# A Mamba-and-experts layer on one core: two chunks' head products in one group

## The chip, the core and the metric

The kernel runs on one core of a Trainium2 chip. Its engines work at the same time and wait for each other by semaphores: TensorE (PE, matrix products into PSUM; its weight loads are listed apart as PEld), VectorE (DVE), ScalarE (ACT), GpSimd (POOL) and SyncE (SP, which here only issues DMAs). PSUM has eight banks of 128 partitions by 512 numbers; a product is written into a bank by PE and read out by DVE or ACT before the bank can be used again. The metric is the device time of one execution in microseconds. A run's "span" is the time from the first to the last instruction in the profile.

## What is computed

Eight sequences of 2048 tokens with 256 features go through one layer: a state-space mixer (Mamba-2) behind a modulated layer norm, then a dense mixture of eight experts behind another. All is float32. Cut to what matters here:

```python
h = _layernorm(x) * (1 + ca) + sa
zxbcdt = h @ W_in                       # z: 512, xBC: 768, dt: 8 columns
xBC = silu(causal_conv4(xBC))           # x: 8 heads of 64, B: 128, C: 128
dt = softplus(dt + dt_bias); A = -exp(A_log)
# the scan, in chunks; cs = cumsum(dt * A) in a chunk
y_diag = sum_j (C_i . B_j) exp(cs_i - cs_j) [j <= i] dt_j x_j
y_off  = exp(cs_i) C_i . S_prev          # S_prev: state that earlier chunks left
S      = exp(cs_last) S_prev + sum_j B_j exp(cs_last - cs_j) dt_j x_j
y = (y_diag + y_off + x * D) * silu(z)
x = x + ga * ((y * rsqrt(mean(y * y) + EPS) * norm_w) @ W_out)
h = _layernorm(x) * (1 + cb) + sb
w = softmax(h @ gate_w + gate_b); w = w * (w >= 0.1); w = w / sum(w)
x = x + gb * sum_e w_e * (h @ expert_w[e] + expert_b[e])
```

The kernel may take its own chunk length, since the result doesn't depend on it: it uses 128 tokens.

## The kernel before

**Tiling.** The tokens are cut into 32 blocks of 512 (`n`), four to a sequence. A block has four chunks of 128 tokens (`c`). Feature-major tiles (features on partitions, tokens along the free axis) serve the projections and the convolution, token-major ones the norms and the experts. The state of a sequence is handed from chunk to chunk in `carry["state"]`.

**Emission.** The order in which instructions are written down comes from a plan: every stage of a block is a Python generator that is put on a list of events at a planned time, in estimated microseconds, and each `yield t` puts the rest of it `t` later on that list. `run()` takes the events in order. `PERIOD` is 70, so stages of several blocks interleave: while block n is projected, the output product of block n-1 and the experts of blocks n-2 and n-3 are written down between its parts. `STARTS` gives each stage's start within its block's plan. The planned times only decide the order; on the chip each engine runs its own queue in order and waits where an operand is missing. The framework under it may still exchange independent instructions on an engine, so the order that counts is that of the built program.

**PSUM.** `take(use, count)` gives a bank that the plan holds to be free and waits in the plan otherwise; `MOST` limits how many banks one use may hold (experts "ex" 3, projections "pj" 2, head products "y" 1, the rest "m" 4). `give` frees it 3.0 planned us later. On the chip the next writer waits for the last reader's semaphore.

**The stages of a block.**
- `fetch` (L241) issues the load of the block's tokens on SP (L105), into one of four buffers; a buffer is free when the store of its earlier block (L737) has landed. `first_norm` takes the statistics (L315, L316 on DVE); `modulated` computes 1/sqrt on POOL (L310, L311), the shift on DVE (L324), the normalised rows on ACT (L328), their transposes on PE (L338) and the modulation on ACT (L340).
- `project_xbc`: six groups of two products of 512 columns (L409); for each, `conv` takes the bank, ACT does the first tap (L364) and saves the last three columns (L368), DVE does the other three taps (L372). `silu_xbc` (L427) follows.
- `steps_of_time`: dt's products, which use 32 columns of the array (L459); softplus and the cumulative sum on DVE and ACT (L471 to L489); `cs` goes to DRAM (L492); dt, cs and e are transposed to token-major by PE (L497) and read out by DVE (L502).
- `project_z`: four groups (L445), read out by ACT with a SiLU (L432).
- `spread` loads, for each chunk, cs of all heads on all partitions (L512, SP) into half of a tile `wide`.
- `within`, for each chunk: ACT writes relu(cs differences) for each head into the other half of `wide` (L526), PE transposes x and B (L536, L537) and makes C.B (L539), ACT takes exp of both halves in one instruction of 2048 columns (L540). DVE makes `xdt` (L543), `sm`, `bm` and the decayed scores `w` (L561), POOL `xdec` (L556) and `cw` (L564). When the state of the chunk before is there, PE does the head products (L579): for each of eight heads `xdt` by `w`, then `state` by `cw`. A head has 64 columns, so such a product uses half of the array's columns, and the two heads of a pair go to the two halves. All of them go to one PSUM bank. Then come the chunk's contribution to the state (L587, full width), the state's update on POOL (L590) and DVE (L609, L607), and the read-out of y: four DVE instructions that add D x (L600), one that multiplies by the gate (L603), the square on ACT (L616) and two sums on POOL (L618, L619).
- `output` sums the squares over partitions on PE (L633), takes 1/sqrt, and does the output product per chunk (L648); `residual` adds it on DVE (L657) with new statistics.
- `gate_weights`: second norm, the gate's logits (L675, 32 columns of the array), a transpose (L683), the softmax and threshold on DVE, and the transpose of the weights `wt` (L714).
- `experts`: bias (L750), then for each chunk four groups of two products of 512 columns (L761); `weighted` adds each expert's part on DVE (L724). After the last one POOL scales and adds the result to the rows (L732, L734), and SP stores the block (L737).

## Time and profile before

| | us |
|---|---|
| median of 4 runs | 2453.53 |
| lowest and highest | 2449.8, 2457.21 |
| the profiled execution | 2451.29 |
| its span | 2449.5 |
| granted TensorE clock, mean | 0.994 |

| group | count | busy us | mean ns |
|---|---|---|---|
| L761 experts, PE | 2048 | 966.1 | 596 |
| L409 projection xBC, PE | 768 | 366.6 | 600 |
| L579 head products, `wide` by `xdt`, PE | 2048 | 142.5 | 281 |
| L579 head products, `cw` by `state`, PE | 1920 | 127.0 | 274 |
| L724 weighting of experts, DVE | 1024 | 485.2 | 476 |
| L600 y plus D x, DVE | 512 | 178.8 | 349 |
| L603 y times gate, DVE | 128 | 87.1 | 681 |
| L540 exp, 128x2048, ACT | 128 | 244.3 | 1908 |
| L564 `cw`, POOL | 128 | 350.6 | 2739 |

How to read it: a float32 product is listed as two records on PE, and records overlap, since a matmul's shown end lies after the start of the next one; so the sum of the means is more than the time they take, and the step from start to start is what counts. "128*64" in a record is the part of the array that is used (rows by columns), "128x512" the output. A row of waits reads: who waited (engine, what it writes, line), for whom, us in total, how often, the longest. "Issue" means that nothing in the profile held the engine back.

### The profile page before, as it was taken

How to read it: one execution, taken by the hardware profiler on the slowest of the kernel's cores; microseconds unless marked ns; L12 is line 12 of the kernel's file. 1: busy time of each engine (PE TensorE's matmuls, PEld its weight loads, DVE VectorE, ACT ScalarE, POOL GpSimd, SP SyncE). 2: the span in 40 equal slices, each digit the busy share in tenths (PEclk: the TensorE clock that was granted, in tenths of full speed). 3: DMA queues.
4: the chain of work that ended last, by engine and by line, in shares of the span. 5: the costliest groups of instructions: out<-in, count | busy, mean ns of one | idle time of the engine just before them, and what ended most of it. 6: DMA issues, size and time to landing. Idle time of an engine off the chain costs nothing.

```text
span 2449.5 us, 33770 instructions
## 1 busy us (share of the span) xinstructions
PE 2365.5 (97%) x11602; PEld 1328.5 (54%) x11602; DVE 1845.9 (75%) x4414; ACT 1508.1 (62%) x2739; POOL 1136.0 (46%) x1244
## 2 busy tenths in 40 slices
PE   7899999999999999999999999999999999999998
PEld 4555555555555555555555555555555555555554
DVE  5767787778777787876777777788777777777775
ACT  6766666666666566656666666666666666656630
POOL 3544454444444544544444445444444544454441
PEclk9899999999999999999999999999999999999999
DMA  5101101111111111011111011110111111111100
GB/s 154 44 28 52 46 28 49 48 45 45 44 37 45 44 53 45 28 53 44 45 45 52 29 45 44 53 45 28 53 44 45 45 45 37 45 44 53 36 26 17
DMA packets 64601, 110.51 MB, mean 45 GB/s; under 512 B 7048, under 2 KB 47024, under 8 KB 64432
## 3 DMA queue, kind: packets, MB, share of 16 engines
q1 hardware_dynamic: 64416, 108.35, 13.2%
q8 instruction: 93, 1.52, 0.3%
q14 instruction: 76, 0.62, 0.1%
q10 hardware_dynamic: 16, 0.01, 0.0%
HBM read 89.47 MB, written 18.87 MB: 44 GB/s over the span
## 4 chain that ended last, share of the span: by engine, by line
PE 27%; DVE 24%; ACT 20%; POOL 14%; DMA 7%; issue 3%; ACTq 0%; POOLq 0%; SPq 0%; DVEq 0%
PE bank L761 10%; POOL cw L564 7%; DVE xbc L372 7%; DMA wide<-cs_d 6%; ACT wide L526 5%; PE bank L445 5%; ACT wide L540 5%; DVE res L724 3%; PE bank L579 3%; PE bank L409 3%; DVE bank L600 3%; ACT xn L328 2%; POOL rstd L311 2%; PE bank L750 2%; POOL xdec L556 2%
## 5 line engine op out<-in xcount | busy, mean ns | idle before, releaser
L761 PE MATMUL bank<-we_sb,ht 128*128 128x512 f32 x2048 | 966.1, 596 | 1.4 <-ACT wide L540 1.4
L761 PEld LDWEIGHTS bank<-we_sb,ht 128*128 128x128 f32 x2048 | 375.8, 191 | 385.1 <-issue 367.4
L724 DVE SCALAR_TENSOR_TENSOR res<-bank,wt,res 128x256 f32<-128x256 f32 x1024 | 485.2, 476 | 100.8 <-PE bank L761 83.2
L564 POOL TENSOR_TENSOR cw<-wide,xbc 128x1024 f32<-128x1024 f32 x128 | 350.6, 2739 | 307.1 <-ACT wide L540 235.3
L372 DVE SCALAR_TENSOR_TENSOR xbc<-bank,conv_w_sb,xbc 128x509 f32<-128x509 f32 (+2 forms) x576 | 425.9, 741 | 50.2 <-ACT halo L368 47.9
L526 ACT ACTIVATE wide<-wide,tok_major 128x128 f32<-128x128 f32 x1024 | 325.1, 389 | 189.4 <-DMA wide<-cs_d 167.7
L409 PE MATMUL bank<-ht,w_in_sb 128*128 128x512 f32 x768 | 366.6, 600 | 6.8 <-DVE zs L603 5.6
L328 ACT ACTIVATE xn<-xt,shift,rstd 128x256 f32<-128x256 f32 x256 | 132.9, 589 | 289.8 <-DVE shift L324 289.8
L590 POOL TENSOR_TENSOR state<-state,wide 128x512 f32<-128x512 f32 x112 | 118.7, 1060 | 336.8 <-DVE state L609 301.4
L540 ACT ACTIVATE wide<-wide 128x2048 f32<-128x2048 f32 x128 | 244.3, 1908 | 1.0
L648 PE MATMUL bank<-wo,zs 128*128 128x256 f32 x1024 | 243.7, 382 | 0.0
L600 DVE SCALAR_TENSOR_TENSOR bank<-xbc,d_ch,bank 128x128 f32<-128x128 f32 x512 | 178.8, 349 | 83.2 <-PE bank L579 77.2
L445 PE MATMUL bank<-ht,w_in_sb 128*128 128x512 f32 x512 | 241.2, 593 | 0.0
L648 PEld LDWEIGHTS bank<-wo,zs 128*128 128x128 f32 x1024 | 196.0, 192 | 79.5 <-issue 52.5
L618 POOL TENSOR_TENSOR sq<-sq 128x256 f32<-128x256 f32 x128 | 96.0, 750 | 280.9 <-ACT sq L616 278.7
L409 PEld LDWEIGHTS bank<-ht,w_in_sb 128*128 128x128 f32 x768 | 139.7, 192 | 157.7 <-issue 147.1
L561 DVE TENSOR_TENSOR wide<-wide,sm 128x1024 f32<-128x1024 f32 x128 | 200.3, 1565 | 0.0
L556 POOL TENSOR_TENSOR xdec<-xdt,tok_major 128x512 f32<-128x512 f32 x120 | 138.8, 1157 | 114.4 <-DVE xdt L543 83.3
L364 ACT ACTIVATE xbc<-bank,conv_b_sb,conv_w_sb 128x512 f32<-128x512 f32 x192 | 147.0, 766 | 59.7 <-PE bank L409 59.6
L445 PEld LDWEIGHTS bank<-ht,w_in_sb 128*128 128x128 f32 x512 | 95.7, 192 | 109.0 <-issue 106.4
L579 PEld LDWEIGHTS bank<-wide,xdt 128*64 128x64 f32 x2048 | 110.9, 138 | 68.6 <-issue 32.6
L732 POOL TENSOR_TENSOR res<-res,gates 128x256 f32<-128x256 f32 x128 | 96.1, 751 | 105.2 <-DVE res L724 105.2
(127 smaller groups left out, 3171.3 us busy)
## 6 DMA issues: line engine op xcount, KB each, us to landing
wide<-cs_d SPq DMA_DIRECT2D x128, 512.0 KB
xt<-_attn_hidden_states_dram SPq DMA_DIRECT2D x32, 512.0 KB
out_dram<-xt SPq DMA_DIRECT2D x32, 512.0 KB
we_sb<-in_L_ffn_expert_w_dram SPq DMA_DIRECT2D x8, 256.0 KB
cs_d<-cs SPq DMA_DIRECT2D x32, 64.0 KB
ht<-in_L_wmod_dram SPq DMA_DIRECT2D x2, 512.0 KB
w_in_sb<-in_L_attn_W_in_dram SPq DMA_DIRECT2D x1, 776.0 KB
w_in_sb<-in_L_attn_W_in_dram SPq DMA_DIRECT2D x1, 512.0 KB
```

Of the source, the lines that this page charges most:

```text
L372: nc.vector.scalar_tensor_tensor(acc[:, ahead:], ps[:, : T - ahead], conv_w_sb[:, m, k : k + 1], acc[:, ahead:], ALU.mult, ALU.add,)
L409: nc.tensor.matmul(ps, w_in_sb[:, k, DI + m * P : DI + (m + 1) * P], ht[:, k, :], start=(k == 0), stop=(k == KD - 1),)
L445: nc.tensor.matmul(ps, w_in_sb[:, k, ts(m, P)], ht[:, k, :], start=(k == 0), stop=(k == KD - 1),)
L526: nc.scalar.activation(wide[:, 1, h, :], wide[:, 0, h, :], AF.Relu, bias=tok_major[:, 1, c, h : h + 1])
L540: nc.scalar.activation(wide, wide, AF.Exp, scale=-1.0)
L556: nc.gpsimd.tensor_tensor(by_head(xdec), by_head(xdt), per_head(tok_major[:, 2, c, :]), ALU.mult)
L561: nc.vector.tensor_tensor(w, w, sm[:, None, :].to_broadcast([P, NH, P]), ALU.mult)
L564: nc.gpsimd.tensor_tensor(cw, up_to, ct_[:, None, :].to_broadcast([P, NH, P]), ALU.mult)
L600: nc.vector.scalar_tensor_tensor(y[:, m, :], xbc[:, m, tok], d_ch[:, m : m + 1], y[:, m, :], ALU.mult, ALU.add)
L648: nc.tensor.matmul(o_ps[:, :DM], d["zs"][:, m, ts(c, P)], wo[:, m, :], start=(m == 0), stop=(m == MI - 1),)
L724: nc.vector.scalar_tensor_tensor(res, ps[:, ts(q, DM)], wt[:, c, e + q : e + q + 1], res, ALU.mult, ALU.add)
L761: nc.tensor.matmul(ps, ht[:, k, ts(c, P)], we_sb[:, k, e : e + per, :].rearrange("p e o -> p (e o)"), start=(k == 0), stop=(k == KD - 1),)
```

## The change

The head products leave `within` and move into a new generator `outputs`, which is started behind every second chunk and handles both chunks of the pair. It takes two PSUM banks at once and writes down all head products of the first chunk and then of the second, one behind the other; then the read-out of the first bank and that of the second, with the same instructions as before. The state's contribution and update of a chunk now come ahead of its head products. `wide` is cut in two tiles: `wide` (two buffers) and `w` (three), so that exp becomes two instructions of 1024 columns. `xdt` and `cw` have three buffers, `state` four.

In the plan, the transposes of dt come 3.0 later, the transpose of the gate's weights 2.5 later, the sum of squares 3.5 later, `fetch` starts 8 later, `gate_weights` 4 later and `experts` 9 later.

```diff
-    MOST = {"ex": 3, "pj": 2, "y": 1, "m": 4}
+    MOST = {"ex": 3, "pj": 2, "y": 2, "m": 4}
...
         nc.scalar.activation(e, cs, AF.Exp, bias=whole)
-        yield 4.0
+        yield 7.0
         t_ps = yield from take("m")
...
-        wide = info[n]["wide", c] = new(chk, [P, 2, NH, P], "wide")
+        wide = info[n]["wide", c] = new(chk, [P, NH, P], "wide")
...
+        w = new(chk, [P, NH, P], "w", bufs=3)
         for h in range(NH):
             nc.scalar.activation(
-                wide[:, 1, h, :], wide[:, 0, h, :], AF.Relu, bias=tok_major[:, 1, c, h : h + 1]
+                w[:, h, :], wide[:, h, :], AF.Relu, bias=tok_major[:, 1, c, h : h + 1]
             )
...
         nc.scalar.activation(wide, wide, AF.Exp, scale=-1.0)
+        nc.scalar.activation(w, w, AF.Exp, scale=-1.0)
         yield 1.2
-        xdt = new(chk, [P, DI], "xdt")
+        xdt = new(chk, [P, DI], "xdt", bufs=3)
...
-        cw = new(chk, [P, NH, P], "cw")
-        nc.gpsimd.tensor_tensor(cw, up_to, ct_[:, None, :].to_broadcast([P, NH, P]), ALU.mult)
+        cw = new(chk, [P, NH, P], "cw", bufs=3)
+        nc.gpsimd.tensor_tensor(cw, wide, ct_[:, None, :].to_broadcast([P, NH, P]), ALU.mult)
...
         if not last:
 
             st_ps = yield from take("m")
             nc.tensor.matmul(st_ps[:, :DI], bm, xdec, start=True, stop=True)
-            behind = new(blk, [P, DI], "state", bufs=3)
+            behind = new(blk, [P, DI], "state", bufs=4)
...
         d["state", c] = True
+        d["parts", c] = [(xdt, w)] if state is None else [(xdt, w), (state, cw)]
+        yield 1.5
         if not last:
             if state is None:
                 nc.vector.tensor_copy(behind, st_ps[:, :DI])
             else:
                 nc.vector.tensor_add(behind, st_ps[:, :DI], behind)
             give(st_ps)
...
+        if c % 2:
+            yield 1.5
+            yield from outputs(n, c - 1)
+
+    def outputs(n, first):
+
+        d = info[n]
+        xbc, g = d["xbc"], d["zs"]
+
+        pair = yield from take("y", 2)
+        for j, y_ps in enumerate(pair):
+            parts = d["parts", first + j]
+            for i, (lhs, rhs) in enumerate(parts):
+                for h in range(NH):
+                    m, q = divmod(h, 2)
+                    nc.tensor.matmul(
+                        y_ps[ts(q, HEADDIM), ts(m, P)], lhs[:, ts(h, HEADDIM)], rhs[:, h, :],
+                        start=(i == 0 and m == 0), stop=(i == len(parts) - 1),
+                        skip_group_check=True,
+                    )
+        yield from until(d, *(("z_silu", m) for m in range(MI)))
+        for j, y_ps in enumerate(pair):
+            c = first + j
+            tok = ts(c, P)
+            yield 1.4
+            y = y_ps.rearrange("p (m t) -> p m t", m=MI)
+            for m in range(MI):
+                nc.vector.scalar_tensor_tensor(
+                    y[:, m, :], xbc[:, m, tok], d_ch[:, m : m + 1], y[:, m, :],
+                    ALU.mult, ALU.add,
+                )
+            nc.vector.tensor_tensor(g[:, :, tok], y, g[:, :, tok], ALU.mult)
+            give(y_ps)
+            yield 1.8
...
@@ def output
         wo = gated[b][0]
+        yield 3.5
         s_ps = yield from take("m")
...
@@ def gate_weights
         nc.vector.tensor_mul(w, w, over(wsum))
-        yield 4.0
+        yield 6.5
...
-        (fetch, -20.0), (first_norm, -9.0), (project_xbc, 11.5), (project_z, 42.0),
-        (silu_xbc, 47.5), (output, 128.0), (gate_weights, 151.0), (experts, 183.0),
+        (fetch, -12.0), (first_norm, -9.0), (project_xbc, 11.5), (project_z, 42.0),
+        (silu_xbc, 47.5), (output, 128.0), (gate_weights, 155.0), (experts, 192.0),
```

The lines of the changed kernel that the text names: L608 head products (before L579), L576 the state's contribution (L587), L579 and L590 its update (L590, L609), L620 and L624 the read-out of y (L600, L603), L740 the weighting (L724), L777 the experts (L761), L748, L750 and L753 the result and its store (L732, L734, L737), L527 the relu (L526), L541 and L542 the two exps (L540), L565 `cw` (L564), L664 the output product (L648), L691, L699 and L730 the gate's products and transposes (L675, L683, L714).

## The prediction, made before the changed kernel had run

> **What bounds the kernel now.** I read the page's busy shares first, then the stretch between fill and drain by windows, then the waits of TensorE, then its timeline.
>
> ```profile
> PE 2365.5 (97%) x11602; PEld 1328.5 (54%) x11602; DVE 1845.9 (75%) x4414; ACT 1508.1 (62%) x2739; POOL 1136.0 (46%) x1244
> 200.00:2380.00 2180.00, 2134.15 (x10564) 1198.90 (x10563) 1669.96 (x4007) 1358.55 (x2469) 1032.38 (x1113) 1.00 0.13 44
> PE bank L497 <- DVE xbc L372: 23.8, 29, 1.5
> PE bank L714 <- DVE wt L710: 11.1, 14, 1.6
> PE bank L338 <- DVE zs L603: 6.0, 10, 0.8
> PE bank L409 <- DVE zs L603: 5.6, 13, 0.7
> ```
>
> TensorE (PE) is the bound. Between 200 and 2380 us it is busy 2134.15 of 2180 us at clock 1.00, so 45.9 us are idle, and the four rows of waits (total, times, longest) make 46.5 us over the whole run: nearly all of it. Nothing else waits long enough to matter; the 75% of DVE counts only where it ends these four waits. So two things can move the time: the time that the same matmuls take, and these stops.
>
> The timeline shows what a matmul costs (start, shown length, records). Shown lengths overlap; the step from one start to the next is the cost.
>
> ```profile
> 1209.88 1.88 PE L761 MATMUL bank<-we_sb,ht 128*128 128x512 f32 x4
> 1211.60 1.89 PE L648 MATMUL bank<-wo,zs 128*128 128x256 f32 x8
> 1213.42 1.09 PE L579 MATMUL bank<-wide,xdt 128*64 128x128 f32 x16
> 1214.44 1.13 PE L587 MATMUL bank<-xdec,bm 128*128 128x512 f32 x2
> 1215.41 1.88 PE L761 MATMUL bank<-we_sb,ht 128*128 128x512 f32 x4
> 1217.12 1.89 PE L648 MATMUL bank<-wo,zs 128*128 128x256 f32 x8
> 1229.18 0.64 PE L459 MATMUL bank<-ht,w_dt 128*32 128x128 f32 x16
> 1229.76 1.09 PE L579 MATMUL bank<-wide,xdt 128*64 128x128 f32 x16
> 1230.68 1.04 PE L579 MATMUL bank<-cw,state 128*64 128x128 f32 x16
> 1231.66 1.13 PE L587 MATMUL bank<-xdec,bm 128*128 128x512 f32 x2
> 1232.62 1.88 PE L761 MATMUL bank<-we_sb,ht 128*128 128x512 f32 x4
> ```
>
> The column 128*64 is the width of the array that is used. Between full-width groups eight L648 records take 1.72 us and four of L761 1.71 to 1.72. Ahead of a narrow group the eight take 1.82. Sixteen narrow records would take 0.875 (two halves of the array at once, 0.109 a pair: the four transposes of L536 take 0.43 to 0.44); the first sixteen take 0.92 and the last sixteen of a group 0.98. L587, half of 1.72, should take 0.86 and takes 0.96 to 0.97 behind a narrow group. Medians over all such places: 0.093 + 0.045 us to go narrow, 0.093 + 0.103 us to come back: 0.139 and 0.196. L459 shows the same (0.58 for 0.44 of work), and narrow to narrow (L459 to L579) costs 0.141.
>
> **The change, part by part.**
>
> *Grouping.* No matmul is added or removed (6458 in both programs). I counted changes of width along PE's order in both: into narrow from full 164, after 134; back 164, after 134; narrow to narrow 32, after 1. It is not half of them, because the new groups no longer sit next to L459's and L675's narrow groups, which now go in and out alone. Saving 30 x 0.139 + 30 x 0.196 + 31 x 0.141 = 4.2 + 5.9 + 4.4 = **14.4 us**. The groups of two are whole in the new order (four runs of eight, one behind the other). If a change of width were only moved into a weight load, the saving would be 0; each piece above is a step between starts, so I take all of it.
>
> *The stop at L497.* The wait names the last tap of the convolution, not dt:
>
> ```profile
> 1242.41 0.60 PE L338 MATMUL bank<-ident,xn 128*128 128x128 f32 x4
> 1244.09 0.30 PE L497 MATMUL bank<-ident,dt 128*128 128x128 f32 x1 [1.08 <-DVE xbc L372]
> 1243.21 0.74 DVE L372 SCALAR_TENSOR_TENSOR xbc<-bank,conv_w_sb,xbc 128x511 f32<-128x511 f32 x1
> ```
>
> dt was ready (L483 at 1239.24); what lacked is the PSUM bank, which L497 takes over from L409 and which DVE still read until 1243.95. DVE has no gap from 1232.67 to there. A stop costs its idle time and the 0.16 us by which a shown end (1.88) passes the step (1.72): L497 23.8 + 29 x 0.16 = 28.4; L714 11.1 + 2.2 = 13.3; the two rows behind L603 (the bank of y, read by L600 and L603) 11.6 + 23 x 0.16 = 15.3. Together 57 us, 2 us a block.
>
> What follows by the new order, in us after L459: L497 goes from 13.6 to 16.8 (an expert group, 1.72, and more stand ahead of it). But the two y now end side by side, and all eight L600 and both L603 (L620, L624 in the new lines) lie in DVE's queue ahead of that tap. The tight place becomes the expert group just ahead of L497 (L777, at 15.1 in three blocks of four, 14.2 in the fourth): its bank is freed by the second L740 (L724 before) of an earlier expert group. DVE's queue from the first tap to there, in steps of the rows of before: 5 L372 x 0.66, 4 L724 x 0.40, 8 L600 x 0.33, 2 L603 x 0.60, the state's add 0.60, L481 1.03, L486 0.76, L487 0.73, five short ones 0.91: 12.7 us. The first tap starts 3.49 after L459 now (1232.67). With that, DVE is there at 16.2: a stop of 1.1 us, 1.9 in the fourth block, 1.3 on average. The tap waits for ACT, which first does four L328 (xn), which wait for L324 and POOL's L311, and now POOL does a cw (2.36 us) ahead of that; in the new order it does not, and the tap could start about 1.1 us earlier: stops of 0 and 0.9, 0.2 on average. Between the two I take 0.75 x 29 = **22 us** of new stops (6 to 38).
>
> L714: from the head's transpose L683 to L714 the new PE order holds 11.2 us, before 10.3, and the convolution is further on; DVE's own queue reaches wt about 1 us ahead of PE. I take its 13.3 as gone (to half of it left: +7). The y banks: their next users (two L338 groups) stand at 14.7 and 17.2 us, L624 ends at about 12 and 13.4, so 2.7 and 3.8 us to spare: 15.3 gone. Stops then: -57 + 22 = **-35 us**.
>
> "PSUM — Partial Sum Buffer" of the Trainium skill, in its summary of rules for kernel authors, says to evacuate promptly because PSUM is tight, which speaks against a second bank held for y. If the second bank stopped PE as often as the one bank does now, both sets of 15.3 us would stand and the sum would be -19 instead of -49. The trace has one such bank without slack (L603 ends at 1238.7 us, about as L338's turn comes); the new order gives both banks more, so I go by the order.
>
> *Exp in two instructions (L540).* One of 2048 columns takes 1.91 us; two of 1024, by L427's row (128x1024, 1.05), 2.10: 0.19 x 128 = 24 us of ACT. The new order also has 223 table loads for 209: 14 x 1.28 = 18 us. ACT goes from 62% to about 65%; its idle 38% hides it. Without that cover it would delay L364 and so the taps, and the 42 us would count at most once: +42.
>
> *State earlier, wide freed earlier.* The state's add leaves the y block and comes some 4 us earlier on DVE; the load of wide no longer waits for L561 and L579 (SP's longest waits). Both only loosen: 0.
>
> *Load of x later (fetch -20 to -12, experts +9).* First statistics L315 wait for the load:
>
> ```profile
> 1194.23 0.39 SPq L737 DMA_DIRECT2D out_dram<-xt  x1
> 1197.20 0.38 SPq L105 DMA_DIRECT2D xt<-_attn_hidden_states_dram  x1
> 1201.15 0.43 DVE L315 BATCH_NORM_STATS2 stats<-xt 128x6 f32<-128x256 f32 x1 [1.70 <-DMA xt<-_attn_hidden_states_dram]
> ```
>
> The store must land (2.97) before the load, and that takes 3.95: 6.9 us. In the new SP order the store stands behind two more wide loads, and in POOL's a cw (2.36) now precedes the last L732 and L734. DVE meets L315 some 6 us after the last weighted sum; the data come 11 after it: a wait of 3 to 5 us a block, up to 2.3 before. Behind it the next bank that PE needs from DVE (for L648) comes 7 us later, so it costs 0; above that slack each us costs 31.
>
> *Fill and end.* The first expert group stands 103.6 us of matmul steps into the program, before 94.7. By 143 us, when it starts now, PE has lost 48 us, some 2 of them in the last ten: 0 to +4, I take 1, half of that rate. At the end PE is busy with experts without a stop, in both orders: 0.
>
> Sum: -14.4 - 35 + 1 = **-48 us**. Against the profiled run of 2451.3 (span 2449.5 and 1.8 around it) that is 2403; the median of the four runs stands 2.2 above, so **2405**.
>
> **The rivals.** (a) *The stop moves and stays.* If DVE is as late at the new place as at the old ones taken together (57 us: the upper 1.9 us in every block), only the widths are gained: 2453.5 - 14.4 = 2439. For it: DVE has no gap for 11 us there, and the change puts more into that stretch. Against: the sum above has DVE late only by 0.2 to 1.3. (b) *Slower: L315 starves DVE.* If the load comes more than 7 us after DVE's turn, L724 and xdt behind it are late, then L648's bank and L587. Ten us late, 3 above the slack: +93 - 48, 2498; slower than before from 8.6 us on. For it: three things delay the store. Against: 3 to 5 us by the rows. (c) *The widths cost as much as before*, because the weight loads hide in the switches: 2419. Against: the steps above.
>
> **How the numbers follow.** A measurement of this kernel tells about 0.2% (5 us) from no change. Forecast (2385 to 2422, with c's 2419 in it) 0.58; lower, all stops gone, 2381, 0.06; (a) and what lies between, 2422 to 2448, 0.18; no change 0.05; (b) and slower 0.13. Faster 0.82. The range goes from 2381 (-14.4 - 57) to 2440, (a)'s end; the forecast's own is 2385 to 2422.
>
> **What would show it.** Right: no row for L497 <- L372 and L714 above 3 us; a new row L777 <- DVE L740 of 6 to 38 us; the last sixteen of the first y 0.875 (no 0.98) where the second follows; DVE L315 waiting 60 to 150 us in total without a PE row behind it; PE's share at 98%. Wrong: PE rows behind DVE L673 or POOL xdec, an ACT row ahead of the taps larger than 47.9 us, or idle time in the first 150 us grown by more than 4.

## The result and the profile after

The changed kernel takes 2457.1 us (median of 37 runs, 2451.3 to 2466.4), the one before 2454.1 in the same comparison (58 runs, 2447.2 to 2459.0). The ratio is 1.0013, with a 95% interval of 1.0007 to 1.0018: 3 us slower, clear of the noise but inside the 0.2% (5 us) that the prediction takes for no change, where 48 us less were forecast. The profiled run has a span of 2459.9 us, the one before 2449.5.

The busy shares of the changed kernel, from its page:

```profile
PE 2361.3 (96%) x11602; PEld 1339.8 (54%) x11602; DVE 1832.9 (75%) x4414; ACT 1541.8 (63%) x2881; POOL 1082.0 (44%) x1244
```

The stretch between fill and drain by windows (busy time of PE, weight loads, DVE, ACT, POOL; then clock, DMA share, GB/s):

```profile
200.00:2380.00 2180.00, 2118.14 (x10462) 1203.09 (x10460) 1647.75 (x3981) 1384.29 (x2583) 971.51 (x1105) 0.99 0.13 43
```

TensorE is idle for 61.9 us of this stretch, before for 45.9. Its waits (total, times, longest):

```profile
PE bank L649 <- POOL sqs L634: 25.6, 23, 3.3
PE bank L699 <- ACT halo L368: 21.3, 22, 1.2
PE bank L730 <- DVE wt L726: 16.7, 21, 1.0
...
PE bank L576 <- POOL xdec L558: 2.6, 3, 0.9
```

Of the four old rows L497 behind the tap and both y banks are gone, as forecast. The wait of the weights' transpose (L714 before, L730 now) has grown from 11.1 to 16.7 us, and the two rows at the top are stops that the prediction doesn't mention: the sum of squares (L649) and the transpose of the head's scores (L699).

To set every term against its forecast I take the steps from start to start of the matmuls. From each I take off the step that the same matmul has behind its like (0.429 us at 512 columns, 0.216 at 256, 0.109 at 128, 0.055 and 0.027 for the narrow forms) and, where the width changes, the prices of the prediction. What is left is listed as a stop, put down to the place where it shows (between 200 and 2380 us where no other stretch is named):

| term, us | forecast | before | after | difference |
|---|---|---|---|---|
| changes of width | -14.4 | 62.5 | 48.0 | -14.5 |
| stop at L497 | -28.4 | 27.6 | 0.5 | -27.1 |
| y banks, L338 and L409 | -15.3 | 17.1 | 0.2 | -16.9 |
| new stop at L777 | +22 | 0.3 | 6.8 | +6.5 |
| weights' transpose, L714, now L730 | -13.3 | 15.2 | 20.5 | +5.3 |
| sum of squares, L649 | not listed | 0 | 28.4 | +28.4 |
| head's transpose, L699 | not listed | 0 | 23.9 | +23.9 |
| L587, now L576 | not listed | 0.5 | 8.7 | +8.2 |
| fill: stops in the first 200 us | +1 | 47.5 | 43.9 | -3.6 |
| ahead of the first and behind the last matmul | 0 | 10.1 | 10.7 | +0.6 |
| rest | | | | -0.4 |
| span | -48 | 2449.5 | 2459.9 | +10.4 |

The gain arrived: 58.5 us, by the first three rows. The first row is a count (360 changes of width before, 269 after) at the prediction's prices, and the prices hold in the new order: a group of 128*64 between full-width ones costs 0.345 us over its work before (32 records) and 0.340 after (64 records), in the median. At the new L777 and the four rows below it 72.3 us were given back, 57.6 of them in the three that top the waits.

**Where L649 comes from.** The timeline of the changed kernel in a block (start, length, what ended an engine's idle time):

```profile
1278.25 2.37 POOL L565 TENSOR_TENSOR cw<-wide,xbc 128x1024 f32<-128x1024 f32 x1 [5.49 <-ACT wide L541]
1278.54 0.63 ACT L631 ACTIVATE sq<-zs 128x512 f32<-128x512 f32 x1
...
1280.57 0.73 POOL L633 TENSOR_TENSOR sq<-sq 128x256 f32<-128x256 f32 x1
1281.39 0.45 POOL L634 TENSOR_TENSOR sqs<-sq 128x128 f32<-128x128 f32 x1
1281.87 0.63 ACT L631 ACTIVATE sq<-zs 128x512 f32<-128x512 f32 x1 [1.75 <-POOL sqs L634]
...
1282.58 0.73 POOL L633 TENSOR_TENSOR sq<-sq 128x256 f32<-128x256 f32 x1 [0.74 <-ACT sq L631]
1283.38 1.32 POOL L634 TENSOR_TENSOR sqs<-sq 128x128 f32<-128x128 f32 x1
1284.75 0.38 PE L649 MATMUL bank<-ones,sqs 128*128 128x1 f32 x2 [1.43 <-POOL sqs L634]
```

The second chunk's square (1281.87) waits for POOL to have added up the first, because `sq` has one buffer; POOL is late with the first, because a `cw` of 2.37 us stands ahead of it in its queue. With one y at a time the squares were 17 to 20 us apart (L616, medians of the four places in a block); now the two of a pair are 2.6 and 3.3.

The stop has a second price. The matmuls that follow the one above, and the window row of the 3.4 us from 1286.3 on (the 0.50 is the granted clock):

```profile
1285.00 2.51 PE L664 MATMUL bank<-wo,zs 128*128 128x256 f32 x8
1287.30 1.92 PE L576 MATMUL bank<-xdec,bm 128*128 128x512 f32 x2
1289.01 2.23 PE L777 MATMUL bank<-we_sb,ht 128*128 128x512 f32 x4
```

```profile
1286.30:1289.70 3.40, 3.40 (x7) 1.75 (x6) 1.71 (x5) 3.37 (x5) 2.79 (x4) 0.50 0.00 0
```

The two records of L576 take 1.71 us from start to start of the next group, where two of 512 columns take 0.86 at full clock. Between 200 and 2380 us the clock is halved in seven such pieces, 27.3 us together, and each piece begins within 2 us of an L649 stop of 1.3 to 2.5 us; the steps in them are 13.3 us longer than their like. The kernel before has no such piece in this stretch. So 13.3 of what the table lists as stops is slower work and no wait: 3.8 in the row of L576, 3.3 in that of L777, and 6.2 at L649 and the output products (L664) behind it. By this estimate the profiled run would have had a span of 2446.6 us at full clock in this stretch, 2.9 below the one before.

**Where L699 comes from.** First the kernel before at the copy of the head's scores, then the changed one:

```profile
1325.54 0.64 PE L675 MATMUL bank<-ht,gate_w_sb 128*32 128x128 f32 x16
1326.25 0.27 ACT L681 COPY head<-bank 128x128 f32<-128x128 f32 x1 [2.73 <-PE bank L675]
1327.31 2.44 ACT L526 ACTIVATE wide<-wide,tok_major 128x128 f32<-128x128 f32 x8 [0.79 <-DMA wide<-cs_d]
```

```profile
1325.99 0.99 ACT L527 ACTIVATE w<-wide,tok_major 128x128 f32<-128x128 f32 x3 [2.49 <-DVE tok_major L502]
...
1327.58 1.58 ACT L527 ACTIVATE w<-wide,tok_major 128x128 f32<-128x128 f32 x5
...
1328.62 0.65 PE L691 MATMUL bank<-ht,gate_w_sb 128*32 128x128 f32 x16
...
1329.19 1.06 ACT L541 ACTIVATE wide<-wide 128x1024 f32<-128x1024 f32 x1
1330.15 1.04 ACT L542 ACTIVATE w<-w 128x1024 f32<-128x1024 f32 x1
1331.10 0.76 ACT L364 ACTIVATE xbc<-bank,conv_b_sb,conv_w_sb 128x512 f32<-128x512 f32 x1
1331.76 0.25 ACT L697 COPY head<-bank 128x128 f32<-128x128 f32 x1
...
1332.07 0.33 PE L699 MATMUL bank<-ident,head 128*128 128x128 f32 x1 [0.88 <-ACT halo L368]
1332.11 1.53 DVE L372 SCALAR_TENSOR_TENSOR xbc<-bank,conv_w_sb,xbc 128x509 f32<-128x509 f32 x2 [1.42 <-ACT halo L368]
```

Before, ACT was idle when the gate's products ended, copied them 0.07 us later, and only then began the rectifiers of the next block's first chunk, which were waiting for the load of `wide`. Now `wide` is there early, so eight rectifiers and both exponentials, some 4.5 us, go ahead of the copy, which comes 2.5 us after the products. L364, ACT's tap of the convolution, is behind them too, so the tap L372 waits 1.42 us, and the weights (L726), which are 10 us further down DVE's queue, are late at L730. This order is that of the built program: eight rectifiers and one or both exponentials stand between L340 and the copy in 29 of the 32 blocks, none in 31 before. ACT's wait for the load fell from 167.7 us to 30.9; DVE's wait for ACT at the taps rose from 47.9 to 105.8.

### The profile page after: what moved, and what is told of

Same layout as the page of the kernel before. It is cut to its first block, busy times and chain, and to the rows that moved or that the text cites. A ratio compares the mean times of both kernels' runs of the same rounds, so it can differ in the third digit from the quotient of the medians.

```text
span 2459.9 us, 33647 instructions
## 1 busy us (share of the span) xinstructions
PE 2361.3 (96%) x11602; PEld 1339.8 (54%) x11602; DVE 1832.9 (75%) x4414; ACT 1541.8 (63%) x2881; POOL 1082.0 (44%) x1244
## 4 chain that ended last, share of the span: by engine, by line
PE 36%; DVE 22%; ACT 21%; POOL 11%; DMA 5%; issue 2%; ACTq 0%; POOLq 0%; DVEq 0%
PE bank L777 14%; PE bank L664 9%; DVE xbc L372 8%; ACT w L527 5%; POOL cw L565 5%; DVE res L740 4%; DVE w L562 4%; DMA wide<-cs_d 3%; PE bank L409 3%; ACT wide L541 3%; ACT L541 3%; ACT xbc L364 2%; PE bank L576 2%; ACT xn L328 2%; PE bank L608 2%
## 5 line engine op out<-in xcount | busy, mean ns | idle before, releaser
L777 PE MATMUL bank<-we_sb,ht 128*128 128x512 f32 x2048 | 959.2, 595 | 0.1
L777 PEld LDWEIGHTS bank<-we_sb,ht 128*128 128x128 f32 x2048 | 380.6, 191 | 392.0 <-issue 367.1
L740 DVE SCALAR_TENSOR_TENSOR res<-bank,wt,res 128x256 f32<-128x256 f32 x1024 | 487.3, 476 | 83.2 <-PE bank L777 71.9
L372 DVE SCALAR_TENSOR_TENSOR xbc<-bank,conv_w_sb,xbc 128x511 f32<-128x511 f32 (+2 forms) x576 | 426.2, 741 | 107.1 <-ACT halo L368 105.8
L565 POOL TENSOR_TENSOR cw<-wide,xbc 128x1024 f32<-128x1024 f32 x128 | 303.7, 2373 | 279.8 <-ACT wide L541 241.8
L527 ACT ACTIVATE w<-wide,tok_major 128x128 f32<-128x128 f32 x1024 | 319.6, 390 | 97.8 <-DVE tok_major L502 53.7
L409 PE MATMUL bank<-ht,w_in_sb 128*128 128x512 f32 x768 | 368.4, 602 | 0.7 <-ACT ht L340 0.7
L579 POOL TENSOR_TENSOR state<-state,wide 128x512 f32<-128x512 f32 x112 | 120.7, 1078 | 422.0 <-DVE state L590 362.9
L620 DVE SCALAR_TENSOR_TENSOR bank<-xbc,d_ch,bank 128x128 f32<-128x128 f32 x512 | 177.7, 349 | 118.8 <-PE bank L608 109.9
L664 PE MATMUL bank<-wo,zs 128*128 128x256 f32 x1024 | 255.1, 393 | 0.0
L340 ACT ACTIVATE ht<-bank,mod_pp 128x512 f32<-128x512 f32 x128 | 95.3, 774 | 223.6 <-PE bank L338 223.5
L409 PEld LDWEIGHTS bank<-ht,w_in_sb 128*128 128x128 f32 x768 | 139.6, 192 | 146.4 <-issue 135.0
L664 PEld LDWEIGHTS bank<-wo,zs 128*128 128x128 f32 x1024 | 193.2, 196 | 37.9 <-issue 16.5
L562 DVE TENSOR_TENSOR w<-w,sm 128x1024 f32<-128x1024 f32 x128 | 206.3, 1612 | 0.0
L364 ACT ACTIVATE xbc<-bank,conv_b_sb,conv_w_sb 128x512 f32<-128x512 f32 x192 | 146.8, 765 | 45.4 <-PE bank L409 45.4
L315 DVE BATCH_NORM_STATS2 stats<-xt 128x6 f32<-128x256 f32 x256 | 104.3, 419 | 94.3 <-DMA xt<-_attn_hidden_states_dram 90.0
L748 POOL TENSOR_TENSOR res<-res,gates 128x256 f32<-128x256 f32 x128 | 93.5, 730 | 168.8 <-DVE res L740 168.4
L631 ACT ACTIVATE sq<-zs 128x512 f32<-128x512 f32 x128 | 80.3, 628 | 99.6 <-POOL sqs L634 95.9
```

The lines of the kernel that those rows point to most:

```text
L364: nc.scalar.activation(acc, ps, AF.Identity, bias=conv_b_sb[:, m : m + 1], scale=conv_w_sb[:, m, HALO : HALO + 1],)
L372: nc.vector.scalar_tensor_tensor(acc[:, ahead:], ps[:, : T - ahead], conv_w_sb[:, m, k : k + 1], acc[:, ahead:], ALU.mult, ALU.add,)
L409: nc.tensor.matmul(ps, w_in_sb[:, k, DI + m * P : DI + (m + 1) * P], ht[:, k, :], start=(k == 0), stop=(k == KD - 1),)
L527: nc.scalar.activation(w[:, h, :], wide[:, h, :], AF.Relu, bias=tok_major[:, 1, c, h : h + 1])
L562: nc.vector.tensor_tensor(w, w, sm[:, None, :].to_broadcast([P, NH, P]), ALU.mult)
L565: nc.gpsimd.tensor_tensor(cw, wide, ct_[:, None, :].to_broadcast([P, NH, P]), ALU.mult)
```

## The experiments

Each line below ran against the kernel before on the same chip, the experiments with four to six runs; the last two columns are the same accounting, widths over the whole program and stops between 200 and 2380 us. The stops hold the slower steps at half clock: 43.2 us in e3, 34.0 in e13, 13.3 in the changed kernel, 8.0 in e6, 6.2 in e2, 1.6 in e8, 1.5 in e1, and none in the others.

| run | median, us | ratio to before | 95% interval | widths | stops |
|---|---|---|---|---|---|
| changed kernel | 2457.1 | 1.0013 | 1.0007 to 1.0018 | 48.0 | 90.1 |
| e1 second buffer for the squares | 2431.4 | 0.9909 | 0.9896 to 0.9922 | 48.0 | 63.7 |
| e2 gate earlier | 2442.1 | 0.9958 | 0.9945 to 0.9972 | 47.7 | 74.0 |
| e3 grouping without the moves | 2580.7 | 1.0514 | 1.0500 to 1.0528 | 49.8 | 185.6 |
| e4 moves without the grouping | 2430.2 | 0.9902 | 0.9889 to 0.9915 | 68.9 | 31.4 |
| e5 e1, exponentials behind the copy | 2392.3 | 0.9753 | 0.9739 to 0.9766 | 48.0 | 26.1 |
| e6 e1, copy on DVE | 2436.1 | 0.9928 | 0.9915 to 0.9942 | 48.1 | 68.4 |
| e7 e5, weights' transpose later | 2385.2 | 0.9722 | 0.9708 to 0.9735 | 47.6 | 17.4 |
| e8 e1, x loaded as early as before | 2433.5 | 0.9921 | 0.9908 to 0.9935 | 48.0 | 65.6 |
| e9 e1, dt as early as before | 2419.4 | 0.9864 | 0.9845 to 0.9883 | 47.6 | 50.6 |
| e10 e7, dt later still | 2395.5 | 0.9764 | 0.9748 to 0.9779 | 47.6 | 28.6 |
| e11 e7, dt as early as before | 2400.8 | 0.9790 | 0.9777 to 0.9804 | 47.9 | 31.9 |
| e12 e4, weights' transpose later | 2411.2 | 0.9828 | 0.9815 to 0.9841 | 61.5 | 21.7 |
| e13 e1, one buffer for wide | 2617.7 | 1.0672 | 1.0658 to 1.0687 | 49.2 | 212.6 |
| e14 e7, rectifiers behind the copy too | 2395.2 | 0.9759 | 0.9745 to 0.9772 | 47.6 | 27.8 |

### e1: the squares' buffer

```diff
-            sq = new(chk, [P, MI, P], "sq", bufs=1)
+            sq = new(chk, [P, MI, P], "sq", bufs=2)
```

> The changed kernel with a second buffer for the squares (sq), nothing else. Theory 1 (the loss is three separate stops, and the largest, L649 behind POOL's L634 with 25.6 us, exists because the second chunk's square waits for the one buffer that POOL is still adding up from the first): ACT's wait at L631 falls from 95.9 us to under 10, the L649 row from 25.6 to under 6, and the time falls by 20 to 28 us, to 2429 to 2437 against 2457. Rival 2 (POOL's queue itself is late, cw and the decay ahead of L634; the buffer is not what decides): the wait at L631 goes but L649 keeps 15 us or more, time 2445 to 2457. Rival 3 (the time moves to the next stop): the L649 row goes, other PE rows grow by as much, time within 5 us of 2457.

Waits of TensorE in e1:

```profile
PE bank L699 <- ACT halo L368: 23.2, 22, 1.6
PE bank L730 <- DVE wt L726: 16.7, 21, 1.0
PE bank L649 <- POOL sqs L634: 6.0, 6, 3.3
```

Theory 1: one more buffer takes 25.7 us off, and L649 falls from 25.6 to 6.0 while the other two rows stay about as they were. In the profiled runs, which are 31 us apart, 12 us of the gain are clock: one piece at half clock is left of seven, and with it 1.5 us of 13.3. What is left of L649 has no wait of ACT at L631 behind it any more: the row behind POOL's L634 is gone.

### e2: the gate's start

```diff
-        (silu_xbc, 47.5), (output, 128.0), (gate_weights, 155.0), (experts, 192.0),
+        (silu_xbc, 47.5), (output, 128.0), (gate_weights, 151.0), (experts, 192.0),
```

> The changed kernel with the gate's start where the kernel before had it (151 for 155), so that the copy of the head's scores (L697) stands ahead of the two exponentials of chunk 0 in ACT's queue again. Theory 1 (L699's 21.3 us come from that queue order alone): the row L699 behind ACT falls under 4 us; L730 gets less PE work between itself and L699 (9.5 for 11.2 us by the steps), so its row stays at 17 or grows, to 15 to 35 us; L649 is untouched (23 to 28). Time 2435 to 2457. Rival 2 (ACT is late at this place whatever stands ahead: the tap's wait for ACT, 105.8 us, and L730 are the same lateness): L699 goes and L730 grows by 20 us or more, time 2452 to 2465.

Waits of TensorE in e2:

```profile
PE bank L699 <- ACT head L697: 31.8, 22, 1.7
PE bank L649 <- POOL sqs L634: 26.8, 24, 3.3
```

Both theories missed the rows. The earlier products met the rectifiers and L541 instead of both exponentials, so the copy came 2.95 us after them for 2.48, and L699 grew; and L730 had no row at all. The lateness was paid once, at L699, and DVE, which waits 69.4 us for ACT at the taps for 105.8, then had the weights in time. The time lies in theory 1's range, but not for its reason.

### e3 and e4: the two halves of the change

e3 is the changed kernel with the times of the kernel before; e4 the reverse, the kernel before with the new times and one y at a time (the diff of e3):

```diff
-        yield 7.0
+        yield 4.0
...
-        yield 3.5
...
-        yield 6.5
+        yield 4.0
...
-        (fetch, -12.0), (first_norm, -9.0), (project_xbc, 11.5), (project_z, 42.0),
-        (silu_xbc, 47.5), (output, 128.0), (gate_weights, 155.0), (experts, 192.0),
+        (fetch, -20.0), (first_norm, -9.0), (project_xbc, 11.5), (project_z, 42.0),
+        (silu_xbc, 47.5), (output, 128.0), (gate_weights, 151.0), (experts, 183.0),
```

The first is dt's transposes, the second the sum of squares, the third the weights' transpose.

> The changed kernel with the grouping of two chunks, but all moves of dt, of the weights' transpose, of the output's first matmul and of the four start times taken back to those of the kernel before. Theory 1 (the widths give their 14 us with the grouping alone, and the moves decide about the stops): changes of width 265 for 360, so -14 us by steps; L497 behind the tap back, at 24 us or more (less PE work between L459 and L497 than in the changed kernel), L649 earlier in PE's order and so more than 25.6 us; time 2460 to 2500, above the changed kernel. Rival 2 (the moves are what costs): the time is below 2450.

> The kernel before with all the moves of the change (dt's transpose, the weights' transpose, the output's first matmul, the start times), and no grouping. Theory 1 (the stop at L497 goes because dt is later, whether or not the y are grouped; the L649 stop needs two squares side by side): changes of width 399 for 360, so +5 us by steps; L497 under 4 us for 23.8; no PE row behind the sum of squares above 5; time 2420 to 2450, faster than before. Rival 2 (the grouping is needed, or the moves alone bring the L649 and the head's stop): PE rows behind POOL's squares or ACT above 15 us, time 2450 to 2475.

The largest wait of TensorE in e3, and three in e4:

```profile
PE bank L648 <- POOL sqs L634: 112.0, 39, 4.6
```

```profile
PE bank L587 <- POOL xdec L556: 12.4, 18, 2.0
PE bank L684 <- ACT halo L368: 7.3, 6, 1.2
...
PE bank L715 <- DVE wt L711: 1.6, 5, 0.4
```

The grouping alone costs 127 us; without the moves the sum of squares stands so soon behind the second y that its row is over four times as large, and 43 us of e3's stops are slower steps at half clock. Theory 1 had the sign and not the size, and its L497 is missing: with the grouping the stop behind the tap left even with dt at its old place. The moves alone gain 24 us, and L497 has no row behind L372 there either, as theory 1 said. So each half cures L497 by itself, and what the grouping adds to the moves in the changed kernel is 48.0 - 68.9 = -20.9 of widths, 90.1 - 31.4 = +58.7 of stops and 43.9 - 50.8 = -6.9 in the first 200 us: 31 us of loss in the profiled runs, 27 by the medians.

### e5, e6 and e7: one lateness or two

e5 keeps the two exponentials of chunk 0 behind the copy on ACT: an order alone, with the matmuls in the order of e1 but for one block in four, where the weights' transpose and the bias of the experts stand 0.86 us earlier.

```diff
-        nc.scalar.activation(wide, wide, AF.Exp, scale=-1.0)
-        nc.scalar.activation(w, w, AF.Exp, scale=-1.0)
+        if c == 0 and n > 1:
+            with tc.issue_after(info[n - 2]["head"]):
+                nc.scalar.activation(wide, wide, AF.Exp, scale=-1.0)
+                nc.scalar.activation(w, w, AF.Exp, scale=-1.0)
+        else:
+            nc.scalar.activation(wide, wide, AF.Exp, scale=-1.0)
+            nc.scalar.activation(w, w, AF.Exp, scale=-1.0)
...
-        nc.scalar.copy(head, lg_ps[:, :P])
+        d["head"] = nc.scalar.copy(head, lg_ps[:, :P]).ins
```

e6 is e1 with the copy on DVE:

```diff
-        nc.scalar.copy(head, lg_ps[:, :P])
+        nc.vector.tensor_copy(head, lg_ps[:, :P])
```

e7 is e5 with the weights' transpose later in the plan:

```diff
-        yield 6.5
+        yield 8.5
```

> The changed kernel with the second buffer for the squares, and in chunk 0 the two exponentials (L541, L542) kept behind the copy of the head's scores (L697) in ACT's queue; PE's order is the same as without that. Theory 1 (L699 and L730 are one lateness: the exponentials, 2.1 us, stand ahead of both the head's copy and of L364, on which the tap L372 and behind it the weights wait): both rows go, L699 from 23.2 and L730 from 16.7 to under 4 us each, the wait of L372 for ACT from 108 to under 75; stops of about 50 us with what a shown end hides, so 2378 to 2395 for 2431.4. Rival 2 (only L699 comes from the exponentials, L730 is late by DVE's own queue, since PE arrives there earlier by what L699 no longer costs): L699 goes, L730 stays or grows to 17 to 40, time 2400 to 2415. Rival 3 (cw, which POOL makes from the exponential, is now late and stops L576 or L608): new PE rows behind POOL above 15 us, time above 2415.

> The changed kernel with the second buffer for the squares, and the copy of the head's scores made by DVE instead of ACT; the exponentials stay where they are, so the tap's wait for ACT stays. Theory 1 (one lateness of ACT behind both): L699 goes (under 4 us for 23.2), but PE then reaches L730 0.9 us earlier while DVE is no earlier: its row grows from 16.7 to 25 to 45 us, time 2412 to 2430. Rival 2 (two separate causes): L699 goes and L730 stays at 17 or less: 2400 to 2410.

> As the one with the exponentials behind the head's copy, and the weights' transpose two us later in the plan (8.5 for 6.5), which puts one more group of 1.72 us between L699 and L730. Theory 1: L730 was gone already, so nothing more: within 4 us of that run (2378 to 2395). Rival 2: L730 still cost 17 to 40 there and goes here, 2380 to 2392, some 20 us below that run.

The timeline of e5 at the copy (its lines stand two to five further down: L696 is L691, L702 is L697, L543 is L541, L704 is L699, L735 is L730):

```profile
1290.57 0.64 PE L696 MATMUL bank<-ht,gate_w_sb 128*32 128x128 f32 x16
1291.04 0.77 ACT L364 ACTIVATE xbc<-bank,conv_b_sb,conv_w_sb 128x512 f32<-128x512 f32 x1
...
1291.70 0.25 ACT L702 COPY head<-bank 128x128 f32<-128x128 f32 x1
...
1291.90 1.07 ACT L543 ACTIVATE wide<-wide 128x1024 f32<-128x1024 f32 x1
...
1292.97 0.27 PE L704 MATMUL bank<-ident,head 128*128 128x128 f32 x1
```

Waits at the weights' transpose, in e5 and in e6:

```profile
PE bank L735 <- DVE wt L731: 13.7, 22, 0.9
```

```profile
PE bank L730 <- DVE wt L726: 45.9, 29, 2.1
```

The order of two instructions on ACT is worth 39 us (2431.4 to 2392.3): the copy comes 0.5 us after the products, L699 has no row, and DVE's wait at the taps falls from 108.4 to 66.0. e6 takes L699 away too, and gains nothing (2436.1, 5 us more than e1): what was waited for there is waited for at L730, whose row goes from 16.7 to 45.9. So the lateness of ACT that is taken away at L699 alone shows at L730, as theory 1 of e6 said, though its time was 6 us short. How much of the growth is that lateness isn't separated: the copy itself takes 0.28 us on DVE, 9 us in all, ahead of the weights. And theory 1 of e5 claimed too much: L730 kept 13.7 us (18.6 by steps, for 24.3 in e1) with the copy no longer late, so most of the 39 us is L699's. e7 shows that rest to be distance: with 1.7 us more between the two transposes (12.0 to 12.9 us for 9.5 to 11.2) the row goes, and 7 us with it. Some 9 us of stop come back at L497 in e7.

### e8: the load of x

```diff
-        (fetch, -12.0), (first_norm, -9.0), (project_xbc, 11.5), (project_z, 42.0),
+        (fetch, -20.0), (first_norm, -9.0), (project_xbc, 11.5), (project_z, 42.0),
```

> The changed kernel with the second buffer for the squares, and the load of x back at the time of the kernel before (-20 for -12 in the plan); PE's order is the same. Theory 1 (DVE's wait at L315 has slack behind it and costs nothing): the wait falls from 90 us to under 40 and the time stays within 4 us of 2431.4. Rival 2 (the late load costs through DVE's queue): 2400 to 2425. Rival 3 (the load waits for the store whatever the plan says): the wait at L315 stays at 80 us or more, time the same.

Rival 3: DVE's wait at L315 is 88.8 us for 90.0, the time 2.0 us more than e1. The plan's time for the load decides nothing, since it waits for the store; and the runs leave the prediction's reading of it, a wait of 2.9 us a block without a stop of TensorE behind it, as it was.

### e9 to e14: what dt's place and the release of wide do

e9 (on e1) and e11 (on e7) put dt's transposes back to the time of the kernel before; e10 (on e7) has 8.0 in the same place:

```diff
-        yield 7.0
+        yield 4.0
```

e12 is e4 with the edit of e7. e13 is e1 with one buffer for `wide`:

```diff
-        wide = info[n]["wide", c] = new(chk, [P, NH, P], "wide")
+        wide = info[n]["wide", c] = new(chk, [P, NH, P], "wide", bufs=1)
```

e14 is e7 with the rectifiers of chunk 0 put behind the copy in the way of e5:

```diff
-            nc.scalar.activation(
-                w[:, h, :], wide[:, h, :], AF.Relu, bias=tok_major[:, 1, c, h : h + 1]
-            )
+            with contextlib.nullcontext() if c or n < 2 else tc.issue_after(info[n - 2]["head"]):
+                nc.scalar.activation(
+                    w[:, h, :], wide[:, h, :], AF.Relu, bias=tok_major[:, 1, c, h : h + 1]
+                )
```

> The changed kernel with the second buffer for the squares, and dt's transposes (L497) back at the time of the kernel before (4.0 for 7.0): L497 14.7 us after L459 by steps, for 16.8, so that the state's decays (L502) and with them ACT's rectifiers and exponentials of chunk 0 start 2 us earlier. Theory 1 (the move of dt bought the stop at L497 off with the lateness of ACT at L699 and L730): ACT's wait for L502 falls from 58 us, L699 and L730 fall from 23.2 and 16.7 to a sum under 20, and L497 behind L372 is back with 15 to 35 us; time 2420 to 2440, that is, about where it was. Rival 2 (dt's place has nothing to do with L699): L699 stays at 20 or more and L497 is back: 2445 to 2465. Rival 3 (the stop at L497 was gone by the grouping, not by dt's move): L497 under 5 us and L699 smaller: 2395 to 2415.

> The one with the squares' buffer, the exponentials behind the head's copy and the later weights' transpose, and dt's transposes one group later still (8.0 for 7.0; 19.0 us after L459 for 16.8). Theory 1 (what is left at L497, about 9 us with what a shown end hides, goes as the tap gets 2 us more): 2374 to 2382 for 2385.2, no row for L497 behind L372. Rival 2 (the later L502 makes ACT late again, as the first move of dt did): L497 gone, ACT's wait for L502 up by 30 us or more, and rows of 10 us or more at L704 or L735: 2385 to 2400.

> The squares' buffer, the exponentials behind the head's copy, the weights' transpose later (8.5), and dt's transposes back at the time of the kernel before (4.0 for 7.0). Theory 1 (dt's move bought nothing in the grouped order, since with the early dt and the squares' buffer alone no stop at L497 came back): the 8.8 us that are left at L497 go, ACT's rectifiers start 2 us earlier, no new row: 2372 to 2383 for 2385.2. Rival 2 (the exponentials that now wait for the head's copy make dt's place indifferent, and what stood at L497 shows at the next group): 2383 to 2390. Rival 3 (the early dt brings the stop behind L372 back once ACT is no longer late): L497 at 15 us or more, 2395 or above.

> The kernel before with the moves and without the grouping, and the weights' transpose two us later (8.5 for 6.5), so that it no longer stands inside a group of the heads' products: 2329.4 us of matmul steps for 2336.7, and L715's 5 us gone. Theory 1: 2430.2 less 7 to 13, so 2417 to 2424; what the grouping is worth once its stops are mended is then 30 to 40 us (21 less 7 of widths, the rest stops at L587 and L684, which the groups that stand alone have). Rival 2 (the widths cost nothing, only L715's stop counts): 2424 to 2428.

> The changed kernel with the second buffer for the squares, and one buffer for wide instead of two: the load of the next chunk's decays then waits until POOL has read the present one (cw and the state's decay), as in the kernel before, where it waited for the products. PE's order about L699 is the same. Theory 1 (the earlier release of wide, which I had priced at nothing, let ACT's rectifiers and exponentials pass the head's copy): ACT's wait for the load of wide is back (above 100 us, 24.7 now), its wait for L502 goes, the copy follows PE's products at once, L699 falls from 23.2 to under 4 us; L730 keeps 10 to 25 us or goes; 2395 to 2415 for 2431.4. Rival 2 (it is dt's late place, whatever wide does): L699 stays at 15 or more, 2425 to 2440. Rival 3 (late decays stop PE elsewhere, at L576 or L608 behind w or xdec): L699 goes, new rows of 20 us or more, 2420 or above.

> The fastest so far (squares' buffer, exponentials behind the head's copy, later weights' transpose: 2385.2), with the eight rectifiers of chunk 0 behind the head's copy too. Theory 1 (the copy and the taps want ACT first, the rectifiers have time): L497's 8.8 us unchanged (they lie ahead of that place), no new row: 2381 to 2387. Rival 2 (rectifiers and exponentials together, 4.5 us, then delay the next L364 or the exponential of the head's scores): rows behind ACT or at the weights' transpose of 10 us or more, 2392 to 2410.

e9: with dt early L699 falls to 11.0 us of stop for 25.9, L730 rises to 29.7 for 24.3, and L497 has none: 12 us gained, between theory 1 and rival 3. In the changed kernel with the squares mended and nothing else, dt's move costs.

In e11, where the copy is no longer late, the same step back costs 15.5 us. The wait of TensorE that shows it:

```profile
PE bank L338 <- DVE xbc L372: 9.9, 28, 1.2
```

The bank behind the tap is now wanted by the norm's transposes, which stand where L497 stood. So dt's move does what it was seen to do, once the later stop is out of the way; rival 3 had the time and theory 1 the row at L497. e10 is 10 us slower than e7, in rival 2's range and not by its way: ACT waits less for L502 (39.4 us for 49.8), and the stops are at L782 (12.9 us, the expert group, for 5.8) and L771 (7.5 for 0.8). e12 gains 19 us over e4, more than theory 1 had: 7.4 of widths and 9.7 of stops. Against e12, the best without the grouping, e7 is 26.0 us faster: some 14 by widths, 4.3 by stops between 200 and 2380 us, 8.2 by stops ahead of that (50.0 to 41.8). The 14 us belong to the grouping; the rest isn't shown to be its own, since e12's stops on ACT's side (L684 and the bias L751, 3.9 + 1.9 and 4.2 us of waits) were not mended as e7's were.

e13 was to show that the early release of `wide` is what lets ACT's work pass the copy. L699 fell from 22 places to 7. ACT at the copy in e13, and its wait for the load:

```profile
1416.86 0.64 PE L691 MATMUL bank<-ht,gate_w_sb 128*32 128x128 f32 x16
...
1417.64 0.26 ACT L697 COPY head<-bank 128x128 f32<-128x128 f32 x1
...
1421.31 2.44 ACT L527 ACTIVATE w<-wide,tok_major 128x128 f32<-128x128 f32 x8 [3.34 <-DMA wide<-cs_d]
```

```profile
ACT w L527 <- DMA wide<-cs_d: 486.5, 112, 10.4
```

The time is rival 3's, with 186 us, since one buffer makes every chunk wait. But the order at the copy answers theory 1: by the number of `wide`'s buffers alone, the rectifiers and exponentials are behind the copy again in 24 of 32 blocks, and the copy comes 0.14 us after the products in the median, for 2.54 in e1. The seven places that are left at L699 are the seven blocks in which eight rectifiers and the first exponential still stand ahead. What this order is worth in time is read from e5, since the loss elsewhere hides it in e13.

e14 restores the order of the kernel before at the copy and is 10 us slower than e7, rival 2's range: 11.6 us of stop at L773, where the experts' bias waits for the transposed weights (0.8 in e7).

## Why the prediction was wrong

**What held.** The widths: 14.4 forecast, 14.5 found. In the timeline of the changed kernel the sixteen of a y that stand inside the group of four start 0.87 us apart, which the prediction had named as the sign:

```profile
1270.36 1.09 PE L608 MATMUL bank<-w,xdt 128*64 128x128 f32 x16
1271.28 1.04 PE L608 MATMUL bank<-cw,state 128*64 128x128 f32 x16
1272.15 1.04 PE L608 MATMUL bank<-w,xdt 128*64 128x128 f32 x16
1273.03 1.04 PE L608 MATMUL bank<-cw,state 128*64 128x128 f32 x16
```

e3 (265 changes of width) and e4 (399) agree: 49.8 and 68.9 us. The stops at L497 and the y banks went, 44 us. That also settles the weighing of "PSUM — Partial Sum Buffer" in the Trainium skill, whose summary of rules for kernel authors says to evacuate promptly: the second bank held for y cost no stop here (L338 and L409 0.2 us for 17.1).

**The failed step: "State earlier, wide freed earlier. Both only loosen: 0."** With a buffer that comes free earlier, the work behind it moved forward in the built order, and in a queue that is worked in order it then stands ahead of something. Here the rectifiers and exponentials went ahead of the copy and of L364: 23.9 us at L699 and a part of the stop at L730. e5 shows by an order alone that the exponentials ahead of the copy cost 39 us. That the release of `wide` put them there is shown by e13, whose one buffer puts them behind the copy again in 24 of 32 blocks.

**"ACT goes from 62% to about 65%; its idle 38% hides it."** ACT gained 33.7 us of busy time for the 42 estimated, and the copy could not use one of its idle microseconds, since ACT's idle time lies ahead of the rectifiers (2.49 us behind L502 in that block) and not behind the copy. The cover was an average over the run, and the wait hung on one place. The sign that the prediction gave for this case, an ACT row ahead of the taps above 47.9 us, is there: 105.8.

**The list of stops lacks L649.** The prediction asked what follows the two y on DVE and in the banks, and not what they share further on: one `sq`, on ACT and POOL. That `sq` has one buffer stands in the kernel, in a loop that now runs twice in a row. It cost 28.4 us by the table, and the halved clock behind it some 7 more in the rows of L576 and L777; e1 takes back 25.7 of the whole. "Perfetto Trace Analysis" of the Trainium skill says in its section on optimization strategy that the same gap, repeating on the engine that should be saturated, can mean too few buffers. For L649 that is so; for L699, which repeats as regularly (22 places), it isn't: there the order on another engine decides.

**"I take its 13.3 as gone", of L714.** The distance from the head's transpose to the weights' transpose was read in one block, 10.3 and 11.2 us. It is the longest of four: by the order of matmuls the other three have 7.75 before, and 9.5, 9.5 and 10.3 after. DVE, which was said to be 1 us ahead, starts 1.42 us late behind the tap, and wants 10.7 us where there are 9.5. e7 gives it 12.0, and the stop goes.

**The stop at L777**, 22 us of the sum with bounds of 6 and 38, is 6.8, of which 3.3 is half clock: under the lower bound, and the row behind L740 that was given as the sign isn't there. The first tap starts 2.33 us after L459 in nine of ten blocks, which is the 1.1 us earlier start from which that bound was worked out; halfway between the bounds was the wrong place.

**The rivals.** (a), new stops as large as the old, had the kind, with the wrong place and too small a size. (b), L315 starving DVE, didn't come: 90.0 us of waiting (60 to 150 forecast), no row of TensorE behind it. (c) fell with the widths. With L649, L699 and L730 mended the change takes 2385.2 us (e7), 20 less than the forecast of 2405, most of it the 16 by which L777 costs less than the 22 of the sum.

**What stays open**: how the time at L699 divides between the early load of `wide` and dt's later place. dt early took 14.9 us off L699 (e9), `wide` late 15 of 22 places (e13). The moves alone put seven rectifiers and no exponential ahead of the copy in 28 of 32 blocks (e4), the grouping alone eight rectifiers and the first exponential in 22 (e3).

## What to carry to other kernels

When a change frees a buffer or an engine earlier, look at what the built order now puts into that time on an in-order queue, and what of the next stage stands behind it; "it only loosens" holds for a wait and not for an order. Ask for every pair of things put side by side which buffers, banks and queues they share all the way to their last reader, and read a distance in every kind of block and not in one. A loss that moves with the fix (e6) has its cause further up: e7, the best version here at 2385.2 us (ratio 0.9722, 0.9708 to 0.9735), is the changed kernel with one more buffer, two instructions put behind a third, and one transpose two microseconds later.

## What the runs showed of the hardware that wasn't expected

The order of ACT's work costs table loads as well as waits: with the exponentials behind the copy ACT has 2869 instructions (e5) for 2883 (e1), with the same computation; the 14 that are missing are table loads, 1.28 us each in the timelines. And the mean granted clock between 200 and 2380 us was lower where TensorE stopped more: 0.98 in e3 and e13 (186 and 213 us of stops), 0.99 in the changed kernel (90), 1.00 in e7 (17). The clock record has it fall to one half for 3.4 us at a time, behind stops of 1.3 to 2.5 us in the changed kernel, and a piece cost some 1.7 us there (13.3 us for 27.3 at half clock). The times of the changed kernel's 37 runs follow the mean clock: 2465.7 us in the median of the two at 0.988, 2451.6 in that of the four at 0.993. Which stops bring the clock down isn't shown: three more L649 stops of 1.3 us come without such a piece, and so do the 29 stops at L497 of the kernel before, of up to 1.5 us.
